# BiMamba2 with FFN on one core: B.C of the next pair computed next to the state's part of the outputs, and three PSUM banks shared by all short-lived tiles

## The chip, the core and the metric
The kernel runs on one core of one Trainium2 chip. The metric is the device time of one execution in microseconds (us), median of the runs shown. The engines are named as the profile names them: PE is TensorE, the matrix engine (PEld its weight loads), DVE is VectorE, ACT is ScalarE, POOL is GpSimd, SP is SyncE, which issues most transfers. Matrix products land in PSUM, which the kernel uses as eight banks; the other engines read them from there.

## The reference
Everything is float32. `x` is 8 sequences of 512 tokens of 256 features.

```python
x = x + bimamba(layernorm(x))          # two directions, joined by Wo, plus bo
x = x + ffn(layernorm(x))              # x W^T + b + (x V_r) C^T, V_r of rank 32

def _mamba2(x, Win, convw, convb, dtb, Alog, Dsk, normw, Wout):
    z, xBC, dt = split(x @ Win)        # 512, 512 + 2*64, 8 columns
    xBC = silu(conv4(xBC) + convb)     # four causal taps per channel
    xs, Bm, Cm = split(xBC)            # 8 heads of 64; 64 states
    dt = softplus(dt + dtb); dA = exp(dt * -exp(Alog))
    h_t = dA_t * h_(t-1) + dt_t * B_t x_t        # per head, 64 x 64
    y_t = C_t . h_t + Dsk * xs_t
    y = y * silu(z)
    y = y * rsqrt(mean(y * y) + 1e-5) * normw
    return y @ Wout
```
The second direction runs on the sequence reversed and is reversed back. The two are concatenated and multiplied by `Wo`.

## The kernel before
The recurrence is done in chunks of 128 tokens. A **pair** (b, c) is chunk c of sequence b forward together with chunk 3-c backward; 8 sequences make 32 pairs, and the main loop (`for i in range(n)`) handles pair `p = pairs[i]` and prepares `q = pairs[i+1]`. Work of other ages is spread over the same iteration: projections and convolutions of the next sequence (`work`, up to four `Block`s), the gates z of later pairs, the normalisation of pair i-1 (`before`), and the last stage of finished chunks (`Tail`: `t` newly begun, `t0` of the iteration before). Nothing chooses the order: the loop body is the order, and `pin()` at its end fixes it on each engine. Only semaphores between engines then move the start of an instruction, those for a free buffer included.

What an iteration does, by the names of its tiles, with the line of the operation:
- `py` (PE L635), outputs of p: first the state's part, `h` against `dec` (32 products of the small form 64*64; none for c = 0, where no state exists yet), then the part within the chunk, `xdt` against `lam` (32 of form 128*64).
- `evict` (DVE L669) adds py to `yg`; `times_gate` (POOL L676) multiplies by silu(z); `square` (ACT L679) and `presum` (POOL) prepare the mean square; `norm_sum` turns it into `ss` (PE L685) and `norm_mean` (ACT L690) reads it, one iteration later.
- `add_state` forms `pst` (PE L655) from B by tokens, `bn`, and the weighted inputs; `new_state` (DVE L664, ACT for c = 0) adds it to the decayed state, which POOL made (L625). c = 3 has none.
- `turn` of q transposes the inputs, `pxs` (PE L580), and ACT copies them out (L582); POOL scales them (L591).
- `cb` of q (PE L601) are the products of B and C, eight of form 64*64, into two tiles, one per direction. `scan` (DVE L569) makes the decays `lam`, and `mix` (DVE L607) multiplies them by cb.
- `Block.project` gives `pp` (PE L413), `tap` (ACT L424) and `convolve` (DVE L431) read it three more times, `silu` (ACT L449) finishes. `gate` gives `pz` (PE L493), `gate_silu` reads it (ACT L501).
- Of a tail: `pm` (PE L731), `residual` (DVE L738), `norm2` makes `xh` (ACT L748), `turn` gives `pxt` (PE L762) and its copy `xT` (ACT L764), `ffn` gives `pf` (PE L769), which DVE adds (L772).

At c = 3 with a pair to follow (`hold`) the second pxs comes later in the order, since the projected inputs it turns are finished in the same iteration. Every second sequence (odd b, c = 2) carries the step sizes of the next two: a logarithm's **series** on DVE (`ratio`, `series`, in tiles `pzu`), their exponentials, decays and transposes (`pdw`, L386 and L387, ACT copies them). `tokenwise_b` turns B of the next sequence into tokens (`pbn`, L466), at the end of c = 2.

The eight banks are one for a constant seed (`p_seed`), three in `p_proj` (pp, pz, pst, some late pm and pf, the later series tiles), two in `p_tr` (pxs, pxt, ss, cb, pdt, pdw, pbn, ptot and the transposes of the normalised input, pxh) and two in `p_y` (py, pm, pf). Within a pool a new tile takes the bank used longest ago, and its first write waits until the last reader of the old tile is through.

Of the kernel before, what the change touches and what calls it, by code (L numbers as in the profile page):

```python
# [14 lines left out]
P = 128  # L15
# [16 lines left out]
def tile_bimamba_ffn(  # L32
# [55 lines left out]
    def ps(p, shape, name):  # L88
        return p.tile(shape, F32, name=name, tag=p.name)


# [191 lines left out]
    def steps_raw(b0):  # L283

        half = L // 2
        pd = ps(p_tr, [P, half], f"pdt_{b0}")
        quarters = [(i, j) for i in range(NSG) for j in range(2)]
        for k in range(NK):
            for n, (i, j) in enumerate(quarters):
                pe.matmul(  # L290
                    pd[32 * n:32 * (n + 1), :], lhsT=wd2[:, k, :],
                    rhs=seq[b0 + i]["xhT"][:, k, j * half:(j + 1) * half],
                    start=(k == 0), stop=(k == NK - 1), skip_group_check=True, tile_position=(0, 32 * n),
                )
# [25 lines left out]
    class Steps:  # L320
# [9 lines left out]
        def ratio(m):  # L330
            pzu = ps(p_proj if m.b0 else p_tr, [P, 2, P], f"pzu_{m.b0}")
            m.z, m.u = pzu[:, 0, :], pzu[:, 1, :]
            dve.tensor_scalar(m.z, m.e, 2.0, None, ALU.add)
            dve.reciprocal(m.r, m.z)
            dve.tensor_tensor(m.e, m.e, m.r, ALU.mult)
            dve.tensor_tensor(m.u, m.e, m.e, ALU.mult)
# [45 lines left out]
    def steps_by_token(b0):  # L382
        g = seq[b0]["g"]
        dt, wl = g.pop("rows")
        pt = ps(p_tr, [P, 2, P], f"pdw_{b0}")
# [14 lines left out]
    class Block:  # L400
# [4 lines left out]

        def project(self, pool_of=None):
# [4 lines left out]
            pp = self.pp = ps(pool_of or p_proj, [P, L], f"pp_{b}_{d}_{blk}")  # L411
            for k in range(NK):
# [60 lines left out]
    class Gates:  # L473
# [12 lines left out]
        def project(self, d, half):  # L486

            cols = slice(self.c0[d] * P, (self.c0[d] + 2) * P)
            pz = self.pz[d, half] = ps(p_proj, [P, 2, 2 * P], f"pz_{self.name}_{d}_{half}")
            for j in range(2):  # L490
# [13 lines left out]

        def project_one(self, d, second):
            n = self.c0[d] + (second if d == 0 else 1 - second)
            pz = self.pz[d, second] = ps(p_proj, [P, NBLK, P], f"pz_{self.name}_{d}_{second}")
# [10 lines left out]
    class Pair:  # L518
# [57 lines left out]
        def turn(m, d, pool_of=None):  # L576

            pt = ps(pool_of or p_tr, [P, DI], f"pxs_{m.name}_{d}")
            for blk in range(NBLK):
# [48 lines left out]

        def outputs(m):

            m.py = [ps(p_y, [P, NBLK, P], f"py_{m.name}_{d}") for d in range(2)]

            def add(d, h, lhsT, rhs, first, last):
                blk, two = divmod(h, 2)
                pe.matmul(  # L635
                    m.py[d][two * HD:(two + 1) * HD, blk, :], lhsT=lhsT, rhs=rhs, start=first, stop=last,
                    skip_group_check=True,
                )

            order = [(d, 2 * blk + two) for blk in range(NBLK) for d in range(2) for two in range(2)]  # L640
            if m.c:
                for d, h in order:
                    rows = slice(d * NS, (d + 1) * NS)
                    add(d, h, m.s["h"][rows, h * HD:(h + 1) * HD], m.dec[rows, h, :], h < 2, False)
            for d in range(2):
                for h in range(NH):
                    add(d, h, m.xdt[d][:, h * HD:(h + 1) * HD], m.lam[d][:, h, :], m.c == 0 and h < 2, h >= NH - 2)

        def add_state(m):
            if m.c == NC - 1:  # L650
                return
            pst = m.pst = ps(p_proj, [P, DI], f"pst_{m.name}")
            for d in range(2):
# [27 lines left out]
        def norm_sum(m):  # L681

            m.ss = ps(p_tr, [P, 2, P], f"ss_{m.name}")
            for d in range(2):
# [20 lines left out]
    class Tail:  # L705
# [15 lines left out]
        def project(t):  # L721
            if t.last:
                t.pm = [ps(p_proj, [P, DM], f"pm_{t.name}_{d}") for d in range(2)]
            else:
                at = begin[ends.index((t.b, t.c))]
                pm = ps(p_proj if at >= n - NC and (t.b, t.c) != (NB - 1, 2) else p_y, [P, 2, DM], f"pm_{t.name}")
                t.pm = [pm[:, d, :] for d in range(2)]
# [31 lines left out]
        def turn(t):  # L759
            pt = ps(p_tr, [P, NK, P], f"pxt_{t.name}")  # L760
            for k in range(NK):
# [4 lines left out]
        def ffn(t):  # L766
            t.pf = ps(p_proj if t.b == NB - 1 and t.c in (0, 3) else p_y, [P, DM], f"pf_{t.name}")
            for k in range(NK):
# [34 lines left out]
    def projected(*key):  # L803
        first[key].project(p_y if key[1] in (2, 3) else None)

# [64 lines left out]
    gates = Gates(0, 0)  # L870
    gates.project_one(0, 0)
    gates.project_one(1, 0)
    steps_by_token(0)
    q.turn(0)
    conv(1, 2)
# [3 lines left out]
    ahead = Block(1, *blocks[0])  # L879
    ahead.project()  # L880
    prepare_wy(0, (0, 1), True)
# [60 lines left out]
    for i in range(n):  # L942
# [32 lines left out]
        if b:  # L975
            p.decay_state()
            if q:
                q.scale_c()
        p.outputs()

        early = q is not None and b == NB - 1
        if early:
            q.scan(0)
        for d in range(2):
            p.evict(d)
            p.times_gate(d)
        p.add_state()
        p.new_state()
        if q:
            q.turn(0)  # L990
            if not hold:
                q.turn(1)
        if hold:
            when(before, "norm_sum", "norm_mean")
            when(late, "silu")
        elif work[0] is not None:
            when(t0, "norm2")
        if i in (1, 2):

            work[0].project(p_y)  # L1000
        when(work[0], "project" if i > 2 else None, "tap")
        if hold:
            if work[0] is None:
                gate(0)
            q.turn(1)
        if not q:
            when(t[:1], "bias1", "project")
        when(t0, "turn")
        if not hold:
            when(before, "norm_sum", "norm_mean")  # L1010
# [4 lines left out]
        if not hold and b:  # L1015
            when(late, "silu")
        if st and not even and c == 2:
            st.exponential()
        if q:
            if not hold or work[0] is not None:  # L1020
                gate(0)
            q.cb()
            gate_silu(0)
            if i == 0:
                steps_last(0)
# [11 lines left out]
        if q:  # L1037
            q.mix(0)
            q.mix(1)
        if st and not even and c == 2:  # L1040
            st.decays()
# [8 lines left out]
        p.presum()  # L1050
        if st and not even and c == 2:
# [14 lines left out]
        if even and c == 2 and ahead + 1 < NB:  # L1066
            scales1(ahead + 1)
        when(work[1], "project", "tap")
        if not hold and not b:
            when(late, "silu")  # L1070
        if i == 0:
            prepare_wy(1, (2, 3), True)
        elif i == 1:
# [9 lines left out]
        if q:  # L1083
            for j in (1, 2, 3):
                gate(j)
                gate_silu(j)
        if even and c in (1, 3) and ahead < NB:
# [4 lines left out]
        if i == 0:  # L1092
            steps_total(0)
# [14 lines left out]
        when(work[3], "convolve_aside")  # L1108
        if st and not even and c == 2:
            steps_by_token(ahead)  # L1110
            st = None
        late, before = work[2:] if i else work[1:], p
# [70 lines left out]
```

## Time and profile before
| | us |
| --- | --- |
| three runs | 618.14, 621.55, 620.36 |
| their median | 620.36 |
| the profiled execution | 619.29 |
| its span, first to last instruction | 617.5 |
| PE busy in it | 596.7 (97%) |
| DVE busy | 545.9 (88%) |
| POOL busy | 460.9 (75%) |
| ACT busy | 412.2 (67%) |

The granted TensorE clock is 0.993 on the mean. All times of single instructions come from the profiled execution. A line of the timeline gives start, length, engine, line, operation and tiles (out <- in), the number of instructions joined in it, and in brackets how long the engine had been idle and who released it. Instructions on PE overlap, so that the distance from one group's start to the next one's says more than a group's length. A line of the waits gives the waiting engine with its tile and line, the releaser, microseconds in total, how often, and the longest.

### The profile page before, as it was taken

The numbers are of one execution on the slowest core, as the hardware profiler recorded it, in microseconds if no ns is written. First come the engines' busy times: TensorE is split into PE (matmuls) and PEld (weight loads), VectorE is DVE, ScalarE is ACT, GpSimd is POOL, SyncE is SP. The second block draws the span as 40 slices with busy tenths as digits, with TensorE's granted clock in tenths as the row PEclk, the third lists the DMA queues.
The fourth block names the chain that finished last, engine by engine and source line by source line (L and its number), as shares of the span: only waits on it lengthen the run. The fifth ranks groups of instructions, "written<-read, shape, count | busy, mean of one in ns | idle before, by whom it ended". The sixth has DMA issues, their size and how long they took to land.

```text
span 617.5 us, 11937 instructions
## 1 busy us (share of the span) xinstructions
PE 596.7 (97%) x4316; PEld 428.3 (69%) x4316; DVE 545.9 (88%) x826; ACT 412.2 (67%) x949; POOL 460.9 (75%) x559
## 2 busy tenths in 40 slices
PE   5989999999999999999999999999999999999996
PEld 2467677677676776766767677767767767777784
DVE  5887988889999989988999998888999998888963
ACT  3688786867676576785786766775877755565531
POOL 3287885777857897776859799677967889499972
PEclk9999999999999999999999999999999999999998
DMA  7475340026064423108026422305206442444011
GB/s 223 139 227 197 111 106 7 2 83 192 4 197 153 120 86 102 37 5 257 19 84 186 129 73 86 121 20 189 54 6 191 120 120 87 121 120 120 18 52 35
DMA packets 36250, 64.80 MB, mean 105 GB/s; under 512 B 8608, under 2 KB 23392, under 8 KB 36192
## 3 DMA queue, kind: packets, MB, share of 16 engines
q1 hardware_dynamic: 34048, 64.00, 34.1%
q8 instruction: 34, 0.56, 0.4%
q10 hardware_dynamic: 2144, 0.04, 0.2%
q14 instruction: 24, 0.20, 0.1%
HBM read 59.12 MB, written 4.72 MB: 103 GB/s over the span
## 4 chain that ended last, share of the span: by engine, by line
PE 65%; DVE 19%; ACT 6%; POOL 5%; issue 3%; DMA 2%; SPq 0%; DVEq 0%; POOLq 0%; ACTq 0%
PE pp L413 16%; PE pm L731 12%; PE pz L493 12%; PE py L635 9%; DVE lam L569 5%; DVE xc L431 4%; PE pf L769 4%; PE pxs L580 4%; PE pst L655 2%; DVE lam L607 2%; DVE yg L669 1%; PE cb L601 1%; DVE x L738 1%; PE pz L510 1%; DMA dec__1431<-dec 1%
## 5 line engine op out<-in xcount | busy, mean ns | idle before, releaser
L431 DVE SCALAR_TENSOR_TENSOR xc<-pp,conv_sb,xc 128x511 f32<-128x511 f32 x180 | 133.4, 744 | 25.9 <-ACT xc L424 21.7
L413 PE MATMUL pp<-xhT,win_sb 128*128 128x512 f32 x320 | 151.5, 600 | 1.0 <-ACT v L278 0.5
L569 DVE TENSOR_TENSOR_SCAN lam<-lam,seed 128x512 f32<-128x512 f32 x128 | 145.6, 1197 | 0.0
L676 POOL TENSOR_TENSOR yg<-yg,sz 128x512 f32<-128x512 f32 x64 | 80.8, 1284 | 57.5 <-DVE yg L669 49.4
L731 PE MATMUL pm<-wy,yg 128*128 128x256 f32 x512 | 115.8, 379 | 0.0
L493 PE MATMUL pz<-xhT,win_sb 128*128 128x256 f32 x448 | 106.5, 380 | 0.3 <-DVE xc L431 0.2
L731 PEld LDWEIGHTS pm<-wy,yg 128*128 128x128 f32 x512 | 97.0, 190 | 13.4 <-issue 0.3
L493 PEld LDWEIGHTS pz<-xhT,win_sb 128*128 128x128 f32 x448 | 82.4, 190 | 17.9 <-issue 4.5
L413 PEld LDWEIGHTS pp<-xhT,win_sb 128*128 128x128 f32 x320 | 57.9, 192 | 47.1 <-issue 42.5
L615 ACT ACTIVATE yg<-xc,dcol 128x128 f32<-128x128 f32 x256 | 81.0, 393 | 0.0
L424 ACT ACTIVATE xc<-pp,conv_sb 128x512 f32<-128x512 f32 x64 | 49.7, 779 | 43.3 <-PE pp L413 43.2
L607 DVE TENSOR_TENSOR lam<-lam,cb 128x1024 f32<-128x1024 f32 x64 | 74.9, 1211 | 1.7 <-PE cb L601 1.7
L591 POOL TENSOR_TENSOR xdt<-xs,dw 128x512 f32<-128x512 f32 x64 | 66.6, 1045 | 1.1 <-ACT xs L582 1.1
L635 PE MATMUL py<-lam,xdt 128*64 128x128 f32 x1024 | 63.0, 276 | 0.6 <-POOL xs L591 0.6
L582 ACT COPY xs<-pxs 128x512 f32<-128x512 f32 x64 | 35.1, 588 | 39.8 <-PE pxs L580 39.8
L635 PEld LDWEIGHTS py<-lam,xdt 128*64 128x64 f32 x1024 | 55.3, 137 | 8.8 <-issue 2.5
L501 ACT ACTIVATE sz<-pz 128x512 f32<-128x512 f32 x56 | 33.1, 591 | 32.1 <-PE pz L493 31.9
L591 POOL TENSOR_TENSOR xs<-xs,dw 128x512 f32<-128x512 f32 x48 | 50.2, 1045 | 3.8
L669 DVE TENSOR_TENSOR yg<-py,yg 128x512 f32<-128x512 f32 x64 | 41.5, 682 | 9.2 <-PE py L635 5.0
L580 PEld LDWEIGHTS pxs<-ident,xc 128*128 128x128 f32 x256 | 28.2, 141 | 26.8 <-issue 13.4
L679 ACT ACTIVATE sz<-yg 128x512 f32<-128x512 f32 x64 | 38.0, 627 | 9.5 <-POOL yg L676 9.4
L702 POOL TENSOR_TENSOR sz<-sz 128x512 f32<-128x512 f32 x32 | 40.8, 1276 | 0.3 <-ACT sz L679 0.3
(234 smaller groups left out, 944.8 us busy)
## 6 DMA issues: line engine op xcount, KB each, us to landing
lam<-dat SPq DMA_DIRECT2D x64, 512.0 KB
x<-in_x_dram SPq DMA_DIRECT2D x36, 128.0 KB
out_dram<-x SPq DMA_DIRECT2D x32, 128.0 KB
x<-in_x_dram SPq DMA_DIRECT2D x7, 512.0 KB
win_sb<-in_win_dram SPq DMA_DIRECT2D x2, 640.0 KB
win_sb<-in_win_dram SPq DMA_DIRECT2D x2, 512.0 KB
wot<-in_wout_t_dram SPq DMA_DIRECT2D x2, 512.0 KB
v<-raw SPq DMA_DIRECT2D x48, 4.0 KB
```

The source lines that it names most:

```text
L413: pe.matmul(pp, lhsT=win_sb[:, d, k, c0:c0 + P], rhs=s["xhT"][:, k, :], start=(k == 0), stop=(k == NK - 1),)
L424: act.activation(self.acc, self.pp, AF.Identity, bias=self.w[:, 4:5], scale=self.w[:, 3:4])
L431: dve.scalar_tensor_tensor(self.acc[:, to], self.pp[:, of], self.w[:, 3 - j:4 - j], self.acc[:, to], ALU.mult, ALU.add,)
L493: pe.matmul(pz[:, j, :], lhsT=win_sb[:, d, k, blk * P:(blk + 1) * P], rhs=self.s["xhT"][:, k, cols], start=(k == 0), stop=(k == NK - 1),)
L569: dve.tensor_tensor_scan(lam, lam, sd, 0.0, ALU.mult, ALU.add)
L580: pe.transpose(pt[:, blk * P:(blk + 1) * P], m.s["xc", d][:, blk, m.tcol[d]], ident)
L591: pool.tensor_tensor(hb(to), hb(m.xw[d]), dw[:, j, cols].unsqueeze(2).to_broadcast([P, NH, HD]), ALU.mult)
L607: dve.tensor_tensor(m.lam[d], m.lam[d], m.pcb[d].unsqueeze(1).to_broadcast([P, NH, P]), ALU.mult)
L615: act.activation(yg[:, blk, :], m.s["xc", d][:, blk, m.tcol[d]], AF.Copy, scale=dcol[:, d, blk:blk + 1])
L635: pe.matmul(m.py[d][two * HD:(two + 1) * HD, blk, :], lhsT=lhsT, rhs=rhs, start=first, stop=last, skip_group_check=True,)
L676: pool.tensor_tensor(yg, yg, m.gates(d), ALU.mult)
L731: pe.matmul(t.pm[d], lhsT=yg[:, blk, :], rhs=wy[:, d, blk, :], start=(blk == 0), stop=(blk == NBLK - 1),)
```

## The change
1. `outputs` is cut in two. The order around it was: state's part, part within the chunk, evictions and gate product, `add_state`, `new_state`. It is now: state's part, **cb of q**, `add_state`, part within the chunk, `new_state`, evictions and gate product. So pst stands ahead of the part within the chunk on PE, and `new_state` ahead of the evictions on DVE. cb leaves its place behind pz, except in the pair that carries the series (odd b, c = 2); in the first iteration it stands behind pst.
2. All short-lived tiles but cb come from the three banks of `p_proj`: pxs, ss, pxt, pdt and later pdw are now there with pp, pz and pst. The two banks of `p_tr` keep cb, the series tiles (now all of them, as `zu`), pbn, ptot, pxh and the first pxs and pdw. The two numbers that `ps_work` is given have no effect.
3. `norm_sum` and `norm_mean` come ahead of pp in all iterations but the last two (before: behind pxt, except at c = 3), so norm_mean stands ahead of xh and the tap on ACT.
4. At c = 3 the second pxs comes behind pz and pxt instead of behind pp; pdw of the series goes from the end of c = 2 into c = 3, behind pp; the turns of B go from the end of c = 2 to behind pm at c = 3.
5. In the first iterations: silu of late blocks and `steps_total` move, and one set of weight scalings goes from ACT to DVE.

On POOL and SP the instructions keep their order.

```diff
+    def ps_work(shape, name, long, held):
+        return ps(p_proj, shape, name)
...
-        pd = ps(p_tr, [P, half], f"pdt_{b0}")
+        pd = ps_work([P, half], f"pdt_{b0}", 0, 0)
...
-            pzu = ps(p_proj if m.b0 else p_tr, [P, 2, P], f"pzu_{m.b0}")
-            m.z, m.u = pzu[:, 0, :], pzu[:, 1, :]
+            zu = ps(p_tr, [P, 2, P], f"zu_{m.b0}")
+            m.z, m.u = zu[:, 0, :], zu[:, 1, :]
...
-            pt = ps(pool_of or p_tr, [P, DI], f"pxs_{m.name}_{d}")
+            pt = ps(pool_of, [P, DI], f"pxs_{m.name}_{d}") if pool_of else ps_work([P, DI], f"pxs_{m.name}_{d}", 0.5, 0.8)
...
-            m.ss = ps(p_tr, [P, 2, P], f"ss_{m.name}")
+            m.ss = ps_work([P, 2, P], f"ss_{m.name}", 0.3, 1.3)
...
-            pt = ps(p_tr, [P, NK, P], f"pxt_{t.name}")
+            pt = ps_work([P, NK, P], f"pxt_{t.name}", 0.3, 1.0)
...
-        p.outputs()
+        p.outputs_of_state()
+
+        series = st and not even and c == 2
+        if q and i and not series:
+            q.cb()
+        if i:
+            p.add_state()
+        for d in range(2):
+            p.outputs_within(d)
+        if not i:
+            p.add_state()
+        if q and not i:
+            q.cb()
 
         early = q is not None and b == NB - 1
         if early:
             q.scan(0)
+        p.new_state()
         for d in range(2):
             p.evict(d)
             p.times_gate(d)
-        p.add_state()
-        p.new_state()
         if q:
             q.turn(0)
             if not hold:
                 q.turn(1)
+        if not hold and i < n - 2:
+            when(before, "norm_sum", "norm_mean")
         if hold:
             when(before, "norm_sum", "norm_mean")
             when(late, "silu")
         elif work[0] is not None:
             when(t0, "norm2")
-        if i in (1, 2):
-
-            work[0].project(p_y)
-        when(work[0], "project" if i > 2 else None, "tap")
+        if work[0] and i:
+            work[0].project(held=6.0)
+        when(work[0], "tap")
         if hold:
-            if work[0] is None:
-                gate(0)
+            if st and not even:
+                steps_by_token(ahead)
+                st = None
+            gate(0)
+            when(t0, "turn")
             q.turn(1)
...
-        when(t0, "turn")
         if not hold:
+            when(t0, "turn")
+        if i >= n - 2:
             when(before, "norm_sum", "norm_mean")
...
         if q:
-            if not hold or work[0] is not None:
+            if not hold:
                 gate(0)
-            q.cb()
+            if series:
+                q.cb()
             gate_silu(0)
...
+        if c == 3 and b + 1 < NB:
+            tokenwise_b(b + 1)
...
-            prepare_wy(1, (2, 3), True)
+            prepare_wy(1, (2, 3))
...
-        if c == 2 and b + 1 < NB:
-            tokenwise_b(b + 1)
...
-        if st and not even and c == 2:
-            steps_by_token(ahead)
-            st = None
```

More of the change, by code (lines that the diff above doesn't have):

```diff
@@ L384, in steps_by_token @@
         dt, wl = g.pop("rows")
-        pt = ps(p_tr, [P, 2, P], f"pdw_{b0}")
+        pt = ps(p_tr, [P, 2, P], f"pdw_{b0}") if b0 == 0 else ps_work([P, 2, P], f"pdw_{b0}", 0, 0)
         pe.transpose(pt[:, 0, :], dt, ident)
@@ L404, in __init__, with project @@
             self.b, self.d, self.blk, self.s = b, d, blk, seq[b]
-        def project(self, pool_of=None):
+        def project(self, pool_of=None, held=4.0):
             b, d, blk, s = self.b, self.d, self.blk, self.s
@@ L410, in project @@
             c0 = XBC0 + blk * P
-            pp = self.pp = ps(pool_of or p_proj, [P, L], f"pp_{b}_{d}_{blk}")
+            pp = self.pp = ps(pool_of, [P, L], f"pp_{b}_{d}_{blk}") if pool_of else ps_work(
+                [P, L], f"pp_{b}_{d}_{blk}", 1.8, held
+            )
             for k in range(NK):
@@ L488, in project @@
             cols = slice(self.c0[d] * P, (self.c0[d] + 2) * P)
-            pz = self.pz[d, half] = ps(p_proj, [P, 2, 2 * P], f"pz_{self.name}_{d}_{half}")
+            pz = self.pz[d, half] = ps_work([P, 2, 2 * P], f"pz_{self.name}_{d}_{half}", 1.8, 1.3)
             for j in range(2):
@@ L503, in silu, with project_one @@
             )
-        def project_one(self, d, second):
+        def project_one(self, d, second, held=1.3):
             n = self.c0[d] + (second if d == 0 else 1 - second)
-            pz = self.pz[d, second] = ps(p_proj, [P, NBLK, P], f"pz_{self.name}_{d}_{second}")
+            pz = self.pz[d, second] = ps_work([P, NBLK, P], f"pz_{self.name}_{d}_{second}", 1.8, held)
             for blk in range(NBLK):
@@ L627, in decay_state, with add, outputs_of_state, outputs_within @@
                 )
-        def outputs(m):
-            m.py = [ps(p_y, [P, NBLK, P], f"py_{m.name}_{d}") for d in range(2)]
[L633 to L637, printed above, removed]
-                )
[L640 to L647, printed above, removed]
+        def add(m, d, h, lhsT, rhs, first, last):
+            blk, two = divmod(h, 2)
+            pe.matmul(
+                m.py[d][two * HD:(two + 1) * HD, blk, :], lhsT=lhsT, rhs=rhs, start=first, stop=last,
+                skip_group_check=True,
+            )
+        def outputs_of_state(m):
+            m.py = [ps(p_y, [P, NBLK, P], f"py_{m.name}_{d}") for d in range(2)]
+            if m.c:
+                for blk in range(NBLK):
+                    for d in range(2):
+                        for h in (2 * blk, 2 * blk + 1):
+                            rows = slice(d * NS, (d + 1) * NS)
+                            m.add(d, h, m.s["h"][rows, h * HD:(h + 1) * HD], m.dec[rows, h, :], h < 2, False)
+        def outputs_within(m, d):
+            for h in range(NH):
+                m.add(
+                    d, h, m.xdt[d][:, h * HD:(h + 1) * HD], m.lam[d][:, h, :], m.c == 0 and h < 2, h >= NH - 2
+                )
         def add_state(m):
@@ L651, in add_state @@
                 return
-            pst = m.pst = ps(p_proj, [P, DI], f"pst_{m.name}")
+            pst = m.pst = ps_work([P, DI], f"pst_{m.name}", 1.0, 1.2)
             for d in range(2):
@@ L722, in project @@
             if t.last:
-                t.pm = [ps(p_proj, [P, DM], f"pm_{t.name}_{d}") for d in range(2)]
+                t.pm = [ps_work([P, DM], f"pm_{t.name}_{d}", 1.8, 2.0) for d in range(2)]
             else:
                 at = begin[ends.index((t.b, t.c))]
-                pm = ps(p_proj if at >= n - NC and (t.b, t.c) != (NB - 1, 2) else p_y, [P, 2, DM], f"pm_{t.name}")
+                mine = at >= n - NC and (t.b, t.c) != (NB - 1, 2)
+                pm = ps_work([P, 2, DM], f"pm_{t.name}", 3.5, 2.0) if mine else ps(p_y, [P, 2, DM], f"pm_{t.name}")
                 t.pm = [pm[:, d, :] for d in range(2)]
@@ L766, in ffn @@
         def ffn(t):
-            t.pf = ps(p_proj if t.b == NB - 1 and t.c in (0, 3) else p_y, [P, DM], f"pf_{t.name}")
+            mine = t.b == NB - 1 and t.c in (0, 3)
+            t.pf = ps_work([P, DM], f"pf_{t.name}", 1.0, 1.0) if mine else ps(p_y, [P, DM], f"pf_{t.name}")
             for k in range(NK):
@@ L803, in projected @@
     def projected(*key):
-        first[key].project(p_y if key[1] in (2, 3) else None)
+        first[key].project(p_y if key[1] in (2, 3) else None, 20.0)
     def tap(*key):
@@ L870, in tile_bimamba_ffn @@
     gates = Gates(0, 0)
-    gates.project_one(0, 0)
-    gates.project_one(1, 0)
+    gates.project_one(0, 0, 20.0)
+    gates.project_one(1, 0, 20.0)
     steps_by_token(0)
-    q.turn(0)
+    q.turn(0, p_tr)
     conv(1, 2)
@@ L879, in tile_bimamba_ffn @@
     ahead = Block(1, *blocks[0])
-    ahead.project()
+    ahead.project(held=20.0)
     prepare_wy(0, (0, 1), True)
@@ L978, in tile_bimamba_ffn @@
                 q.scale_c()
-        p.outputs()
+        p.outputs_of_state()
[4 more added lines that the diff above has]
+            p.add_state()
+        for d in range(2):
+            p.outputs_within(d)
[3 more added lines that the diff above has]
+            q.cb()
         early = q is not None and b == NB - 1
@@ L1014, in tile_bimamba_ffn @@
             norm1(ahead + (c == 3))
-        if not hold and b:
+        if not hold:
             when(late, "silu")
-        if st and not even and c == 2:
-            st.exponential()
         if q:
-            if not hold or work[0] is not None:
+            if not hold:
                 gate(0)
-            q.cb()
+            if series:
+                q.cb()
             gate_silu(0)
+            if series:
+                st.exponential()
             if i == 0:
@@ L1039, in tile_bimamba_ffn @@
             q.mix(1)
-        if st and not even and c == 2:
+        if series:
             st.decays()
@@ L1050, in tile_bimamba_ffn @@
         p.presum()
-        if st and not even and c == 2:
+        if series:
             st.weigh()
@@ L1067, in tile_bimamba_ffn @@
             scales1(ahead + 1)
-        when(work[1], "project", "tap")
-        if not hold and not b:
-            when(late, "silu")
+        if work[1]:
+            work[1].project(held=3.0)
+        when(work[1], "tap")
         if i == 0:
-            prepare_wy(1, (2, 3), True)
+            prepare_wy(1, (2, 3))
         elif i == 1:
@@ L1086, in tile_bimamba_ffn @@
                 gate_silu(j)
+        if i == 0:
+            steps_total(0)
         if even and c in (1, 3) and ahead < NB:
@@ L1091, in tile_bimamba_ffn @@
             when(work[2:], "project", "tap")
-        if i == 0:
-            steps_total(0)
         if q:
@@ L1108, in tile_bimamba_ffn @@
         when(work[3], "convolve_aside")
-        if st and not even and c == 2:
-            steps_by_token(ahead)
-            st = None
         late, before = work[2:] if i else work[1:], p
```

## The prediction
> **What bounds the kernel now.** First the page's busy shares, then the waits of TensorE, then the order of time of one quiet pair.
>
> ```profile
> PE 596.7 (97%) x4316; PEld 428.3 (69%) x4316; DVE 545.9 (88%) x826; ACT 412.2 (67%) x949; POOL 460.9 (75%) x559
> ...
> PE 65%; DVE 19%; ACT 6%; POOL 5%; issue 3%; DMA 2%; SPq 0%; DVEq 0%; POOLq 0%; ACTq 0%
> ```
> TensorE is busy 97% of the span and is 65% of the chain that ended last; VectorE (DVE) follows. The waits of TensorE for another engine are few:
>
> ```profile
> PE pf L769 <- ACT xT L764: 1.5, 4, 0.5
> PE pxt L762 <- ACT xs L582: 1.1, 3, 0.6
> ```
> Each line: who waited for whom, microseconds in total, times, the longest. These two lead the list but for the start, where the first transposes wait 6.4 us; none reaches 2 us. So the bound is TensorE's own stream, and an edit pays by what it takes out of that stream or puts between its groups. The timeline of TensorE in the pair (b, c) = (4, 1), start and length ahead of the engine, and below it ScalarE's (ACT's) next to pxs:
>
> ```profile
> 354.89 1.10 PE L635 MATMUL py<-dec__3526,h__3570 64*64 64x128 f32 x32
> 355.93 1.97 PE L635 MATMUL py<-lam,xdt 128*64 128x128 f32 x32
> 357.72 1.03 PE L655 MATMUL pst<-xs,bn 128*64 128x512 f32 x4
> 358.68 1.09 PE L580 MATMUL pxs<-ident,xc 128*128 128x128 f32 x8
> 359.61 1.88 PE L413 MATMUL pp<-xhT,win_sb 128*128 128x512 f32 x4
> 361.33 0.38 PE L762 MATMUL pxt<-ident,xh 128*128 128x128 f32 x2
> 361.55 0.38 PE L685 MATMUL ss<-ident,sz 128*128 128x128 f32 x2
> 361.77 1.89 PE L493 MATMUL pz<-xhT,win_sb 128*128 128x256 f32 x8
> 363.59 0.45 PE L601 MATMUL cb<-cc,bb 64*64 64x128 f32 x8
> 363.97 1.13 PE L769 MATMUL pf<-wf,xT 128*128 128x256 f32 x4
> ```
>
> ```profile
> 359.37 1.08 ACT L582 COPY xs<-pxs 128x512 f32<-128x512 f32 x2 [2.24 <-PE pxs L580]
> 360.33 0.61 ACT L748 ACTIVATE xh<-x,ln_nm,ln_rs 128x256 f32<-128x256 f32 x1
> ```
> Read start against the next start: each group begins as the last one's pipeline allows. From the state's part (dec) to pf it is 9.08 us: dec 1.03, lam 1.80, pst 0.96, pxs 0.93, pp 1.72, pxt 0.22, ss 0.22, pz 1.82, cb 0.38. The same pz takes 1.73 at 368.39, where no cb follows, so entering the 64*64 form costs 0.10; eight cb cover 0.21 of weight loads, so leaving it costs 0.17.
>
> **The change, part by part.**
>
> *cb behind dec.* Both have the form 64*64, so one entry and one exit go: 0.10 + 0.17 = 0.27 us per pair with a state's part. dec, cb, pst, lam, pxs, ss, pp, pxt, pz without waits: 0.86 + 0.38 + 0.86 + 1.90 + 0.93 + 0.22 + 1.72 + 0.22 + 1.73 = 8.82 against 9.08: **-0.26**. In a pair with c = 0 no dec runs; cb enters its form there anyhow and only the change between pz and lam is saved: -0.10.
>
> *Three banks.* Before, the short-lived tiles lay on five banks: pp, pz and pst on three; pxs, pxt, ss and cb on two. Now pst, two pxs, ss, pp, pxt, pz follow each other on three, while two hold only cb, the series and a few early tiles. In the built order each takes the bank of the third one before it. Let S be the start of pxs (358.68 here).
> - pp takes the first pxs's bank. ACT starts its copies at S+0.69, 1.08 for both, so the first is out at about S+1.26. TensorE is through pxs and ss at S+1.15, and a waiting tile follows its reader by about 0.06 (xh ends at 360.94, the weights of pxt, which wait for it, load at 361.00). Wait: **+0.17**, 0 to 0.4.
> - pxt waits on ACT's xh, which now stands behind norm_mean. ACT: copies out at S+1.77, norm_mean 0.86 (362.46 to 363.32), xh 0.61: S+3.24, 3.30 with the 0.06. TensorE is there at S+3.06. From 0 to 0.30; I take **+0.15**, as ACT idled 2.24 us ahead of the copies and can be early.
> - ss takes pst's bank, read by new_state (0.68). That is now first on VectorE and waits for POOL's h (357.68, 1.05 long: out at 358.73): done near 359.4, before ss at S+0.93. Behind it on VectorE the two evictions queue, 0.7 later; POOL's gate product waits for those. At this pair POOL starts it at 361.02, where it was busy until then: 0; the cover gone, it is 0.3 a pair (rival C).
> - pz waits for norm_mean, through before pp ends: 0.
>
> Nine pairs (c = 1 of b = 1 to 6, c = 2 of b = 2, 4, 6): -0.26 + 0.17 + 0.15 = +0.06, **+0.5** in all (-2.3 to +4.0). Six with c = 0: -0.10 + 0.32 = +0.22, **+1.3** (-0.6 to +3.6).
>
> *Odd b, c = 2 and 3.* In c = 2 cb stays behind pz (the series needs a bank of cb's pair). Its three waits, pp and ss on copies and pxt on new_state, come to 0.7; pbn 0.33 and pdw 0.34 leave for c = 3, so the pair c = 2 is neutral. In c = 3 the profile of b = 3 shows:
>
> ```profile
> 322.61 1.88 PE L413 MATMUL pp<-xhT,win_sb 128*128 128x512 f32 x4
> 324.33 0.68 PE L580 MATMUL pxs<-ident,xc 128*128 128x128 f32 x4
> 324.85 0.38 PE L762 MATMUL pxt<-ident,xh 128*128 128x128 f32 x2
> ```
>
> ```profile
> 319.01 4.51 DVE L431 SCALAR_TENSOR_TENSOR xc<-pp,conv_sb,xc 128x511 f32<-128x511 f32 x6
> ```
> This pp (322.61) now takes the bank that the convolution (six instructions, 319.01 to 323.52) still reads: 323.58. Then pp 1.72, pdw 0.34, pz 1.73: pxt at 327.37. The second pxs has pxt's bank, and ACT's copy xT is out 0.8 after pxt began (other pairs: 0.79 to 0.87): pxs 328.2, pf at 328.7. Before, pf stood at 327.27: +1.4, and pbn's 0.33 behind pm: +1.75. Three times (b = 1, 3, 5): **+5.2**. If the convolution comes earlier the wait of 0.97 falls out of it (+0.8 each); if VectorE is later by its new first step, +2.3 each. So +2.4 to +6.9.
>
> *Even b, c = 3* (b = 2, 4). From dec, before: 1.03 + 1.90 + 0.49 + 0.22 + 1.72 + 0.44 + 0.22 + 1.82 + 0.38 = 8.22. After: 0.86 + 0.38 + 1.90 + 0.49 + 0.22 + 1.72 + 1.73 + 0.22 + 0.61 (waiting for xT) + 0.44 = 8.57. **+0.7** for two (0 if a sooner ACT hides xT, -0.5; +1.2 at most).
>
> *Start (b = 0).* The second pxs of the first iteration takes the bank from which ACT copies the first state: +0.95; ACT's silu, moved forward, relieves 0.35. One set of weight scalings goes from ACT to VectorE ahead of the convolutions: +0.65. The next two pairs gain 0.1 and 0.2. **+0.95**, -2 to +3, since TensorE waits some 5 us between 18 and 80 us as it is (0.8 to 1.2 us each ahead of pdt, pdw, pbn and one pz), which a new order may add to or swallow.
>
> *End (b = 7, and the c = 3 of b = 6 that leads into it).* POOL works without a gap from 537 to 593, so there a group's order costs nothing until (7, 2): cb waited 1.16 at 581.05 for ACT's norm_mean, and stands clear behind dec now: pf from 582.58 to about 581.1, -1.5. The last turns share banks and follow their copies in series: +0.4. **-1.1**, -4 to 0.
>
> POOL's and SP's instructions keep their order, so no transfer is issued sooner or later by position.
>
> **Sum:** 0.5 + 1.3 + 5.2 + 0.7 + 0.95 - 1.1 = **+7.6 us**. The profiled execution took 619.29 (span 617.5 and 1.8 around it): 626.9. It is 1.1 under the median of the three runs, 620.36; halfway between the two I say **627.4**.
>
> *A rule against the change.* The row: pp at 359.61 starts right behind pxs, with its bank free, whereas the copies are not out until 360.45. The Trainium skill, "Perfetto Trace Analysis", section "Optimizing Tensor Performance", part "Matmuls", wants independent matmul groups to rotate through different banks so that one's evacuation overlaps the next one's matmuls. By that rule alone the loss would be that of the bank waits, 0.32 x 15 + 5.2 = +10; by the row of the form changes alone it is -0.26 x 9 - 0.10 x 6 = -2.9.
>
> **Rivals.**
>
> *A, faster: the banks are free in time.* Decisive is ACT: if the first copy is out at S+1.1 (0.16 sooner) and xh by S+3.0 (0.3 sooner), neither pp nor pxt waits, since ACT stands idle 2.24 us ahead of the copies. Then -2.3 - 0.6 for the form changes, -2 in the odd c = 2, +2.4 in the odd holds, +0.7 even holds, -1 at the start, -2 at the end: -4.8, **614.5**. Against it: the copy follows pxs by 0.69 whatever ACT did before. 0.21.
>
> *B, no change.* VectorE, 88% busy, paces the pairs around the holds; TensorE's excess there (0.25 before dec, 0.51 before pxs at 321.4) takes up half of what I charge: +5.2 becomes +1.5, the end gains its -2: about +2, **622**, range 617.3 to 623.5. 0.24.
>
> *C, slower still.* New_state first delays both evictions by 0.7; POOL's gate product stood 49.4 us in all waiting for them, and its result feeds square, sum and pm. If 0.3 us of it comes through in 20 pairs, +6 on top: **633**. 0.13.
>
> My forecast, 624 to 631: 0.42. That the change does nothing is excluded: the built order shows every move. Faster or slower by 0.5% is about 3 us, roughly what a measurement of this kernel can tell from none. Chances: faster 0.21, within 0.24, slower 0.55. The range 613.5 to 634 leaves out the ends of A and C.
>
> **What would show it.** In the profile after: pz 1.73 with no cb behind it and cb 0.38 behind dec (else the first part is wrong); pp starting 0.17 after ss, released by ACT's copy; pxt by xh; in the odd c = 3 pp at the convolution's end, and pxs of the hold waiting on xT; TensorE waits for ACT of several microseconds in the list that now has almost none. If pp and pxt start back to back, A holds. If POOL's wait for the evictions rises by some 6 us and py is late, C.

## The result, and the profile after
The changed kernel takes 625.31 us (median of 6 runs, 624.94 to 626.72) against 620.78 for the kernel before in the same measurements (6 runs, 618.14 to 622.69): a ratio of 1.0091, 95% interval 1.0070 to 1.0112. It is slower, by about 5 us; the prediction had said 627.4, with a range of 613.5 to 634. The profiled execution took 624.94, its span is 623.0 against 617.5.

The page of the changed kernel, busy shares and chain:

```profile
PE 594.2 (95%) x4316; PEld 429.0 (69%) x4316; DVE 544.4 (87%) x828; ACT 413.2 (66%) x947; POOL 460.9 (74%) x559
...
PE 58%; DVE 21%; POOL 10%; ACT 7%; issue 3%; DMA 1%; SPq 0%; DVEq 0%; POOLq 0%; ACTq 0%
```
TensorE is busy 2.5 us less in a span 5.5 us longer, and its share of the chain fell from 65% to 58%: it works less and waits more. Not all of the 2.5 us is less work: in the profile before, the granted clock was 0.50 for 3.4 us from 76.83 on, which made the same groups some 1.4 us longer (see the start, below). Its waits for other engines, the two lines behind the start's:

```profile
PE pp L418 <- DVE xc L436: 2.9, 3, 1.0
PE pxs L585 <- ACT xT L773: 2.3, 5, 0.5
```
Neither is in the list of before. They stand for three waits at odd c = 3 and five at c = 3. The pair (4, 1) again, TensorE, and below it ACT next to pxs:

```profile
359.43 1.10 PE L636 MATMUL py<-dec__3526,h__3572 64*64 64x128 f32 x32
360.36 0.40 PE L606 MATMUL cb<-cc,bb 64*64 64x128 f32 x8
360.68 1.08 PE L663 MATMUL pst<-xs,bn 128*64 128x512 f32 x4
361.59 1.92 PE L636 MATMUL py<-lam,xdt 128*64 128x128 f32 x32
363.44 1.09 PE L585 MATMUL pxs<-ident,xc 128*128 128x128 f32 x8
364.37 0.38 PE L693 MATMUL ss<-ident,sz 128*128 128x128 f32 x2
364.77 1.98 PE L418 MATMUL pp<-xhT,win_sb 128*128 128x512 f32 x4
366.60 0.44 PE L771 MATMUL pxt<-ident,xh 128*128 128x128 f32 x2
366.87 1.89 PE L498 MATMUL pz<-xhT,win_sb 128*128 128x256 f32 x8
368.60 1.03 PE L779 MATMUL pf<-wf,xT 128*128 128x256 f32 x4
```

```profile
364.13 1.07 ACT L587 COPY xs<-pxs 128x512 f32<-128x512 f32 x2 [3.30 <-PE pxs L585]
...
365.95 0.59 ACT L757 ACTIVATE xh<-x,ln_nm,ln_rs 128x256 f32<-128x256 f32 x1
```
cb now follows dec and the group lasts 0.32. pz lasts 1.73. But ss, two transposes that took 0.22, holds the stream 0.40, since pp behind it starts at S+1.33, when ACT's first copy is out; pp takes 1.83 where 1.72 is its pace, because pxt behind it waits for xh (366.54); and pxt itself 0.28 for 0.22. That is 0.18 + 0.11 + 0.06 = 0.35. Such short waits are missing from TensorE's own list; they stand in that of its weight loads, where this line is new:

```profile
PEld pp L418 <- ACT xs L587: 5.0, 20, 0.3
```
The wait of pxt's weights for xh is 13.2 us in that list, 7.1 before. From dec to pf it is 9.17, against 9.08 before; pf itself, which no longer follows cb, is 0.10 shorter, so that the whole iteration comes out even.

An iteration can be measured from its first products for p to those of the next. Per kind, from the timelines of the two profiled executions:

| iterations | before | after | difference | forecast |
| --- | --- | --- | --- | --- |
| c = 0, six | 17.72 | 17.99 | +0.27 each | +0.22 |
| c = 1, six | 15.32 or 16.19 | 15.30 or 16.18 | -0.02 | +0.06 |
| c = 2, even b, three | 19.08 | 18.74 | -0.34, of it -0.33 the turns of B | +0.06 without these |
| c = 3, b = 2 and 4 | 19.77 | 20.43 | +0.65, of it +0.33 the turns of B | +0.35 without these |
| c = 2, b = 1, 3, 5 | 21.43, 19.51, 19.30 | 20.82, 19.52, 19.52 | -0.61, +0.01, +0.22 | 0 |
| c = 3, b = 1, 3, 5 | 18.96 | 20.49, 20.39, 20.40 | +1.53, +1.43, +1.44 | +1.75 |
| up to the end of b = 0 | 119.43 | 120.30 | +0.87 | +0.95 |
| (6, 3) and b = 7, to TensorE's last product | 80.80 | 79.66 | -1.14 | -1.1 |

The sum is +5.5, the difference of the spans. The largest part is c = 3 of odd b, in (3, 3) here:

```profile
324.87 0.38 PE L693 MATMUL ss<-ident,sz 128*128 128x128 f32 x2
326.21 1.99 PE L418 MATMUL pp<-xhT,win_sb 128*128 128x512 f32 x4 [0.96 <-DVE xc L436]
...
329.98 0.38 PE L771 MATMUL pxt<-ident,xh 128*128 128x128 f32 x2
330.82 0.66 PE L585 MATMUL pxs<-ident,xc 128*128 128x128 f32 x4 [0.46 <-ACT xT L773]
```
Both brackets are banks: pp's is still read by the convolution, and the second pxs has pxt's.

### The profile page after: what moved, and what is told of

It reads as the page before. It is cut to its first block, busy times and chain, and to the rows that moved or that the text cites. A ratio compares the mean times of both kernels' runs of the same rounds, so it can differ in the third digit from the quotient of the medians.

```text
span 623.0 us, 11918 instructions
## 1 busy us (share of the span) xinstructions
PE 594.2 (95%) x4316; PEld 429.0 (69%) x4316; DVE 544.4 (87%) x828; ACT 413.2 (66%) x947; POOL 460.9 (74%) x559
## 4 chain that ended last, share of the span: by engine, by line
PE 58%; DVE 21%; POOL 10%; ACT 7%; issue 3%; DMA 1%; SPq 0%; DVEq 0%; POOLq 0%; ACTq 0%
PE pp L418 16%; PE pz L498 10%; PE pm L740 10%; PE py L636 7%; DVE xc L436 5%; DVE lam L574 5%; PE pxs L585 3%; PE pf L779 3%; DVE lam L612 2%; PE pst L663 2%; POOL yg L684 2%; DVE yg L677 1%; POOL xs L596 1%; DVE r L345 1%; ACT yg L620 1%
## 5 line engine op out<-in xcount | busy, mean ns | idle before, releaser
L418 PE MATMUL pp<-xhT,win_sb 128*128 128x512 f32 x320 | 153.5, 606 | 4.2 <-DVE xc L436 2.9
L684 POOL TENSOR_TENSOR yg<-yg,sz 128x512 f32<-128x512 f32 x64 | 81.0, 1287 | 64.0 <-DVE yg L677 60.4
L740 PEld LDWEIGHTS pm<-wy,yg 128*128 128x128 f32 x512 | 97.1, 190 | 13.2 <-issue 0.2
L636 PEld LDWEIGHTS py<-lam,xdt 128*64 128x64 f32 x1024 | 57.3, 137 | 15.4 <-issue 13.3
L585 PE MATMUL pxs<-ident,xc 128*128 128x128 f32 x256 | 37.2, 281 | 4.1 <-ACT xT L773 2.3
```

Of the source, the lines that this page charges most:

```text
L418: pe.matmul(pp, lhsT=win_sb[:, d, k, c0:c0 + P], rhs=s["xhT"][:, k, :], start=(k == 0), stop=(k == NK - 1),)
L585: pe.transpose(pt[:, blk * P:(blk + 1) * P], m.s["xc", d][:, blk, m.tcol[d]], ident)
L636: pe.matmul(m.py[d][two * HD:(two + 1) * HD, blk, :], lhsT=lhsT, rhs=rhs, start=first, stop=last, skip_group_check=True,)
L684: pool.tensor_tensor(yg, yg, m.gates(d), ALU.mult)
L740: pe.matmul(t.pm[d], lhsT=yg[:, blk, :], rhs=wy[:, d, blk, :], start=(blk == 0), stop=(blk == NBLK - 1),)
```

## Experiments
The theory (**bank theory**): with three banks in rotation TensorE waits for the last reader of the tile before on the same bank, and for ACT's new order; these waits cost more than cb at its new place saves. Rivals: POOL's gate product is held up by the later evictions (C); cb's place saves nothing; VectorE paces the stretches in which TensorE waits (B). All comparisons of iterations are with the changed kernel's; where a run reached the first pair up to 1.1 us later or 0.4 us earlier, that is left out. The intervals of 2 and 6 overlap that of the changed kernel, so what these two show is shown by the iterations, which agree to 0.05 us where an edit changes nothing ((1, 2) in experiment 2 aside), and not by the total.

**1. cb back behind pz, three banks kept.**
```diff
-        if q and i and not series:
-            q.cb()
...
-            if series:
+            if i:
                 q.cb()
```


> The changed kernel, but cb stands behind pz (at c = 3 behind the second pxs) as before, with the three banks kept. Bank theory with the price of a change of form: +0.27 in nine pairs (c = 1, even c = 2), +0.10 in six with c = 0, +0.27 in two even c = 3, up to 0.5 in three odd c = 3, where the wait for the convolution swallows what leaves the front: +4 to +5 us, about 629.8. Rival (cb at its new place saves nothing, because it only hands the change of form on to pst): no change, 625.3, or faster.

Measured: 631.92 us, ratio to the kernel before 1.0179 (1.0158 to 1.0201). c = 1 and even c = 2 are 0.36 longer each, even c = 3 0.35, c = 0 0.20, odd c = 3 0.58, 0.23 and 0.21, and (6, 3) with b = 7 together 1.0; (1, 2) is 0.44 shorter. Over all iterations that is 6.7 us. So cb's new place saves more than forecast, and the rival falls. TensorE of this kernel in (4, 1):

```profile
370.62 1.89 PE L498 MATMUL pz<-xhT,win_sb 128*128 128x256 f32 x8
372.44 0.45 PE L606 MATMUL cb<-cc,bb 64*64 64x128 f32 x8
372.82 1.13 PE L779 MATMUL pf<-wf,xT 128*128 128x256 f32 x4
373.79 0.38 PE L740 MATMUL pm<-wy,yg 128*128 128x256 f32 x1
```
Start to start: pz 1.82, cb 0.38 and pf 0.97. Behind pz, in the changed kernel, pf takes 0.87. That 0.10 is the part which the forecast missed. Behind pz, cb costs 0.10 in pz, 0.38 itself and 0.10 in pf, 0.58; behind dec, dec and cb take 0.93 + 0.32 = 1.25 where dec alone takes 1.04 here (363.39 to 364.43), 0.21. The difference, 0.37, is the 0.36 of the iterations.

**2. Turns pxt of c = 3 on a bank of py.**
```diff
-            pt = ps_work([P, NK, P], f"pxt_{t.name}", 0.3, 1.0)
+            at = begin[ends.index((t.b, t.c))] + 1
+            held = at % NC == NC - 1 and at < n - 1
+            pt = ps(p_y, [P, NK, P], f"pxt_{t.name}") if held else ps_work([P, NK, P], f"pxt_{t.name}", 0.3, 1.0)
```


> The changed kernel, but the turns pxt of the c = 3 iterations go to a bank of py, so that the second pxs no longer follows them on the same bank. Bank theory (the added time is TensorE waiting for the last reader of the tile before on the same bank): the five waits of pxs for ACT's copy xT (0.6 us each) go, pf then waits about 0.1 for the same copy; each c = 3 iteration of b = 1 to 5 is 0.45 shorter, 2.2 us in all, about 623.1. Rival (the new order on DVE and POOL paces these iterations): those five stay as long as they are, 625.3.

Measured: 624.09 us, ratio 1.0058 (1.0037 to 1.0080). The five iterations are 0.37 to 0.39 shorter, 1.9 in all; (1, 2) ahead of them is 0.25 longer. In (4, 3) the second pxs starts 0.22 behind pxt, where it was 0.84:

```profile
401.14 0.38 PE L773 MATMUL pxt<-ident,xh 128*128 128x128 f32 x2
401.36 0.60 PE L585 MATMUL pxs<-ident,xc 128*128 128x128 f32 x4
401.99 1.13 PE L781 MATMUL pf<-wf,xT 128*128 128x256 f32 x4
```
pf follows 0.63 behind pxs instead of 0.49, since it needs xT itself. So the bank was the cause of the wait of pxs; of its 0.62, 0.38 came back, and the rest became a later pf.

**3. new_state behind the evictions again.**
```diff
-        p.new_state()
         for d in range(2):
             p.evict(d)
             p.times_gate(d)
+        p.new_state()
```


> The changed kernel, but new_state stands behind the two evictions on DVE again. Bank theory: pst's bank is read 1.3 us later and the first pp, which has it now, waits for new_state: about 0.4 us more in each of nine pairs (c = 1; c = 2 of even b), some 0.3 in three of odd b, nothing at c = 0, where ACT makes the new state: about 629.5. Rival (the evictions, 0.7 us later in the changed kernel, hold up POOL's gate product and what follows): POOL's wait for them falls from 60 back to about 50 us and the time by 2 us or more, under 623.5.

Measured: 628.37 us, ratio 1.0123 (1.0106 to 1.0141). c = 1 and even c = 2 are 0.27 longer (0.4 expected), c = 0 unchanged, odd c = 2 0.94 to 0.99 longer (some 0.3 expected), but odd c = 3 0.86 to 0.96 shorter. DVE and TensorE of this kernel in (4, 1):

```profile
365.75 0.69 DVE L677 TENSOR_TENSOR yg<-py,yg 128x512 f32<-128x512 f32 x1 [0.18 <-PE py L636]
366.36 0.68 DVE L672 TENSOR_TENSOR h__3719<-h__3719,pst 128x512 f32<-128x512 f32 x1
```

```profile
367.06 0.41 PE L693 MATMUL ss<-ident,sz 128*128 128x128 f32 x2 [0.33 <-ACT xs L587]
367.31 1.88 PE L418 MATMUL pp<-xhT,win_sb 128*128 128x512 f32 x4
```
The second eviction itself waits for the part within the chunk, and new_state behind it ends at 367.04, S+1.40. In this kernel ss no longer takes pst's bank but the first pxs's, and waits there for ACT's copy until S+1.42; pp, on pst's bank, follows it at S+1.67 instead of S+1.33. So the loss came, but not at the place expected: it is ss that waits, for ACT. Which bank a tile takes is thus not fixed by the order of the tiles alone: it moved when the reader of pst moved. POOL's wait for the evictions, 60.4 us in the changed kernel and 49.4 before, is 60.1 here: it does not come from their place on VectorE, and where it comes from stays open. Rival C falls. New: what odd c = 2 lost, odd c = 3 gave back, where the wait of pp for the convolution went from 2.9 us to 0.8. In this stretch TensorE was ahead of VectorE.

**4. ss and norm_mean behind pxt again.**
```diff
-        if not hold and i < n - 2:
-            when(before, "norm_sum", "norm_mean")
...
-        if i >= n - 2:
+        if not hold:
             when(before, "norm_sum", "norm_mean")
```


> The changed kernel, but ss and norm_mean stand behind pxt again in all iterations but c = 3. Bank theory: pp finds pst's bank free and xh comes before norm_mean, so both waits ahead of pz go; but pz then takes pxt's bank and waits for xT: pz at S+3.8 instead of S+3.43 (c = 1) and S+3.55 (c = 0), S the start of pxs; +0.38 in nine pairs, +0.26 in six, about +5 us, 630. Rival (norm_mean ahead of xh and of the tap on ACT is a loss of its own): the pairs with c = 0 lose their 0.27, the others 0.1 to 0.2, about -2 to -3 us, 623.

Measured: 631.93 us, ratio 1.0179 (1.0160 to 1.0198). c = 1 and even c = 2 are 0.61 longer, c = 0 0.49, odd c = 2 0.61 shorter (b = 1) or 0.69 longer, odd c = 3 0.43 to 1.14 shorter. pp and pxt run without a wait, and the wait has moved to pz, the first line of TensorE's waits:

```profile
PE pz L498 <- ACT xT L773: 12.0, 18, 0.7
```
pz starts at S+3.95 in (4, 1), later than the S+3.8 forecast. Of these two orders that of the changed kernel is the better one for three banks. In both TensorE waits at a bank; norm_mean's place is not the loss. Other orders were not tried.

**5. The first pp on a bank of py, pm on the three, xh ahead of norm_mean** (c = 0 to 2 of b = 1 to 6).
```diff
-            work[0].project(held=6.0)
+            work[0].project(p_y if not hold and b else None, held=6.0)
...
                 mine = at >= n - NC and (t.b, t.c) != (NB - 1, 2)
+                mine = mine or (NC <= at < n - NC - 1 and at % NC < NC - 1)
...
         if not hold and i < n - 2:
-            when(before, "norm_sum", "norm_mean")
+            when(before, "norm_sum")
+            if work[0] is not None:
+                when(t0, "norm2")
+            when(before, "norm_mean")
...
-        elif work[0] is not None:
+        elif work[0] is not None and i >= n - 2:
             when(t0, "norm2")
```


> The changed kernel, but from b = 1 to 6 in the iterations c = 0 to 2 the first pp takes a bank of py (free when the first eviction is through) and pm takes its place on the three banks, and xh comes ahead of norm_mean on ACT. Bank theory: the waits ahead of pp, pxt and pz (0.18 + 0.11 + 0.06 at c = 1 and even c = 2; 0.18 + 0.23 + 0.06 at c = 0) go: 9 x 0.35 + 6 x 0.47 = 6.0 us; what the odd c = 2 gain the odd c = 3 wait longer for the convolution: about 619.3. Rival (TensorE would wait for something else at the same time, VectorE or POOL above all): under 2 us, 623.5 or more.

Measured: 631.82 us, ratio 1.0189 (1.0167 to 1.0212). c = 1 and even c = 2 are 0.34 to 0.35 shorter each, c = 0 0.46 to 0.48: the prices of the waits are those read from the timeline. But odd c = 2 is 5.33, 5.97 and 4.48 longer, 15.8 in all, of which the odd c = 3 behind them give 4.3 back:

```profile
PE pp L418 <- DVE yg L677: 10.1, 3, 4.3
```
In these three pairs VectorE evicts py late: in (1, 2) the series is ahead of new_state (162.86) and the evictions (163.46), and pp waited for them. The forecast of the total had overlooked that. The waits are only 10.1 of the 15.8. Most of the rest is the clock: the granted TensorE clock, 1.00 around these stretches, was 0.50 for 6.8 us from 161.31, for 6.8 us from 311.50 and for 3.4 us from 461.68, the first two times from within the wait on, the third from 0.46 us after it, and pp ran mostly at that clock. In (1, 2):

```profile
164.20 3.78 PE L418 MATMUL pp<-xhT,win_sb 128*128 128x512 f32 x4 [4.30 <-DVE yg L677]
```
From pp to pxt, which starts at 167.77, it is 3.57 here, 3.58 in (3, 2) and 3.16 in (5, 2), where 1.72 is the pace. So these waits of about 3 to 4 us cost half as much again as their own length.

**6. c = 3 of odd b: first pxs and ss on cb's banks, cb behind pxt.**
```diff
+        odd = hold and st and not even
-        if q and i and not series:
+        if q and i and not series and not odd:
             q.cb()
...
-            q.turn(0)
+            q.turn(0, p_tr if odd else None)
...
             when(t0, "turn")
+            if odd:
+                q.cb()
             q.turn(1)
```
and the same bank for `norm_sum` of this iteration.

> The changed kernel, but in the three odd c = 3 iterations (b = 1, 3, 5) the first pxs and ss are on the two banks of cb, and cb follows behind pxt. Bank theory: pp no longer waits for the convolution (0.95), cb fills most of the wait for xT (0.6) but pays its two changes of form again, and pxs waits some 0.3 for its input: -1.1 each, -3.4 in all, about 621.9. Rival (VectorE's convolution paces this stretch whatever the banks): pz or the next pxs wait instead, less than 0.3 each, over 624.4.

Measured: 624.92 us, ratio 1.0079 (1.0059 to 1.0098). pp no longer waits for the convolution, and pf in (3, 3) is 9.0 behind the first products instead of 10.3. But the turns of B, next but one, wait for VectorE's mix on cb's bank:

```profile
335.96 0.55 PE L471 MATMUL pbn<-ident,bb 128*128 128x128 f32 x3 [0.62 <-DVE lam L612]
```
The three iterations are only 0.38 to 0.40 shorter. The total is the one the rival gave: the wait changed its place. But the largest new one stands neither at pz nor at the next pxs; it is again one at a bank, cb's own, which this edit made VectorE read later. Whether VectorE's pace or this order of reads holds the stretch is not separated here.

**7. Edits 2, 5 and 6 together.**


> The three edits together: turns pxt of all c = 3 on a bank of py, the first pp on a bank of py with xh ahead of norm_mean, the odd c = 3 as described. Bank theory: -6.0 - 3.4 - 0.9 (even c = 3) = -10.3 on the changed kernel, about 615, which is under the kernel before. Rival (VectorE, 87% busy, becomes the bound as soon as TensorE stops waiting): about half, 620.

Measured: 628.33 us, ratio 1.0123 (1.0101 to 1.0146). Odd c = 2 is again 4.4 to 6.4 longer, with 10.0 us of waits for the eviction and the clock at 0.50 in the same three pairs; odd c = 3 is 1.8 to 1.9 shorter, the others as in 2 and 5. Edit 5's oversight decides it.

**8. and 9. The same without edit 5 in the three pairs with the series;** in 8 also the turns of B at odd c = 3 behind the pp that followed them, in 9 without edit 6.

> As the kernel with all three edits, but the pairs that carry the series (odd b, c = 2) keep pp on the three banks and pm on a bank of py, as in the changed kernel, since VectorE evicts py 3 to 4 us late there; and at odd c = 3 the turns of B stand behind the pp that followed them, since they waited 0.8 us for mix. Bank theory: 9 x 0.35 + 6 x 0.47 = 6.0 in the pairs c = 0, 1 and even c = 2, as measured one by one; 0.8 in the even c = 3; 1.2 each in the odd c = 3: -10.4 on the changed kernel, about 615. Rival (VectorE paces the stretch c = 2 and 3 of odd b, whatever TensorE saves before it is given back there): only the 0.35 and 0.47 of the even b and the even c = 3 stay, 617.5 to 620.

> The same without the edits of the odd c = 3 iterations: there cb, pxs, ss and the turns of B stay as in the changed kernel. Bank theory: 6.0 + 0.8 + some 0.4 in each odd c = 3: -8.0, 617.3, with the wait of pp for the convolution still there. Rival (VectorE paces c = 2 and 3 of odd b): that wait grows by what the pairs before it saved, 0.8 each, so 619.5 and more.

Measured: 8 takes 617.99 us (12 runs) against 620.11 (23 runs), ratio 0.9960 (0.9942 to 0.9977): 0.4% faster than the kernel before, and about 7 us faster than the changed one. 9 takes 619.78, ratio 0.9997 (0.9982 to 1.0012), no different from the kernel before in these runs. Kernel 8 in (4, 1), without a gap from pxs on:

```profile
360.22 1.09 PE L585 MATMUL pxs<-ident,xc 128*128 128x128 f32 x8
361.15 0.38 PE L693 MATMUL ss<-ident,sz 128*128 128x128 f32 x2
361.37 1.88 PE L418 MATMUL pp<-xhT,win_sb 128*128 128x512 f32 x4
```
In 8, c = 0 is 0.44 to 0.48 shorter than in the changed kernel, c = 1 and even c = 2 0.34 to 0.35, even c = 3 0.4, odd c = 3 1.15 to 1.24. But odd c = 2 is 1.06, 0.72 and 0.45 longer, and there TensorE waits for VectorE's new_state: 1.83 in (1, 2), 0.25 in (5, 2), and in (3, 2):

```profile
307.30 0.41 PE L774 MATMUL pxt<-ident,xh 128*128 128x128 f32 x2 [0.53 <-DVE h__3149 L672]
```
So the bank theory holds for the pairs and for even c = 3; in c = 2 and 3 of odd b VectorE takes back a part of what TensorE saves, and kernel 8 wins only 0.18, 0.43 and 0.71 over the two together. The wait for new_state too is one at a bank, since pxt reads nothing that new_state writes; but here the reader itself is late. Whether another bank would end that wait or only move it was not tried. In 9 odd c = 3 gains 0.28 to 0.38 and odd c = 2 loses 0.72 to 1.13, as the rival had it for the total, though the wait that grew was mostly that of pxt for new_state in c = 2, not pp's for the convolution. Whether new_state could come sooner there was not tried, nor was cb at its new place with the five banks as they were, the most direct test of what cb alone brings.

## Why the prediction was right, point by point
- **The bound.** TensorE's own stream, with few waits: right for the pairs, as each edit moved them by what its groups and waits add up to. Between c = 2 and 3 of odd b VectorE is close behind; the prediction had this only as rival B.
- **cb behind dec, -0.26.** Right in kind, mis-sized: 0.36, and 0.20 instead of 0.10 at c = 0 (experiment 1). The missing 0.10 is in the group behind cb.
- **pp +0.17, pxt +0.15.** Measured 0.18 and 0.17 at c = 1, 0.18 and 0.29 at c = 0, and experiment 5 took them away in full. With the larger saving of cb that makes -0.02 instead of +0.06, and +0.27 instead of +0.22. That c = 0 came so close is luck: the waits were 0.15 larger than forecast and the saving 0.10. (By its own terms TensorE reaches pxt at S+3.04, not S+3.06; nothing hangs on it.)
- **ss at no cost because new_state is first.** Right: behind the evictions it costs 0.27 in each of nine pairs, though by a wait of ss for ACT on another bank (experiment 3).
- **Odd c = 3, +1.75 each.** Right in both waits, 0.96 for the convolution (0.97 forecast) and 0.62 for xT (0.61 forecast, experiment 2). What was too high is their sum, 1.43 to 1.53. In odd c = 2 the pair b = 1 gained 0.61 where 0 was forecast; before, its state's part stood 0.83 us behind a VectorE addition, and in the changed kernel that wait is gone. Both together are 1.2 of the 2.1 us by which the forecast of +7.6 exceeds +5.5.
- **Even c = 3, +0.35; start +0.95; end -1.1.** Measured +0.32, +0.87, -1.14. The agreement at the start is partly luck. In the profile before, the clock of 0.50 from 76.83 to 80.24 falls on pz and pxh of (0, 1): from pz to the next pp it is 4.41 us, in the changed kernel, at full clock, 2.98. Without that stretch the start would have been about 2.3 longer by this estimate, not 0.87. The other runs' mean clocks do not tell whether they have it too. The prediction also misplaced the waits at the start: the two longest, 0.96 each, stand ahead of a pxs and of pwf, and ahead of pdw and pbn there is none. At (7, 2) cb no longer waits for norm_mean; pxt waits 1.16 for new_state in its place, but later in the stream.
- **The rivals.** A would have needed the banks free in time; they were not, but experiment 5 shows that where they are, 0.35 and 0.47 a pair come back, and kernel 8 shows the other sign. B did not come as forecast: odd c = 3 cost 4.4 us in all, not 1.5. That VectorE takes back what TensorE saves shows only at c = 2 and 3 of odd b, and only in part (experiments 3, 8 and 9). C fell in experiment 3, although the sign it named, POOL's wait for the evictions up by 11 us, did appear: that sign told nothing about its cause.
- **The rule.** The waits at the banks and for xh in the pairs are 6.0 us by experiment 5, those at c = 3 some 6.0 (five times 0.62, three times 0.96). Against them stand 6.7 for cb. What "Perfetto Trace Analysis" of the Trainium skill asks for in "Optimizing Tensor Performance", that groups rotate through banks so that reading one overlaps the next, was here the larger half of the account: +10 by the rule alone, near +12 by the waits read, without the saving. The part in the pairs came back in full when the banks were changed; of the 6.0 at c = 3 experiments 2 and 6 brought back 1.9 and 1.2, as other waits took the place of the rest.

## What to carry to other kernels
Count an edit on a saturated TensorE stream twice: what it takes out of the groups, and for each tile who reads the tile before on its bank, and until when; here 6.7 us of saving met some 12 of waits. Bring the tile that is read late (a projection that a convolution reads) to a bank that is free early and not needed soon, and the short ones into the rotation. A wait that goes may come up behind the same engine a few groups later, so look at the whole iteration and not at the bracket, and at which engine is next behind. A long wait can cost more than its length: in experiment 5, 10.1 us of waits came with a halved clock behind them and made three pairs 15.8 us longer.

## What was not expected of the hardware
A group of 64*64 products between 128*128 groups costs more than its own time on three places: 0.10 us in the group before it (pz 1.82 for 1.73), 0.17 beyond its weight loads, and 0.10 in the group behind (pf 0.97 for 0.87). Behind another 64*64 group it adds 0.21 in all, the eight weight loads alone.

The granted clock fell to 0.50 for 3.4 to 6.8 us in or right after each of the three waits of 2.77 to 4.30 us in experiment 5. Waits of 0.92 to 1.83 us, as at 179.67 in the changed kernel or at 163.52 in kernel 8, show no such stretch, with one exception: behind the wait of 0.96 at 75.53 in the kernel before the clock was 0.50 for 3.4 us. What sets this one apart is not known.
